# A Performer stage of four interleaved blocks: another order of the steps, and the rotation's sum on another engine

## The chip, the cores and the metric

The kernel runs on one core of a Trainium2 chip. The metric is the device time of the whole program in microseconds (us). A core has five engines that run their own instruction streams in order and meet at semaphores: TensorE (PE, matmuls into PSUM banks; PEld is its weight load), VectorE (DVE), ScalarE (ACT), GpSimd (POOL) and SyncE (SP, which issues the transfers).

## The reference, cut to what matters

A small hybrid network runs on 8 images of 128 channels and 16x16 pixels: an adder convolution, a layer of state-space scans with convolutions, a layer of attention with a mixture of experts, and a Performer of eight layers with a spectral filter at the end. The change lies in the Performer's attention. For each layer, of 8 heads with 16 channels:

```python
q = (t @ Wq[i] + bq[i]).reshape(Bb, N, H, DH).transpose(0, 2, 1, 3)
k = (t @ Wk[i] + bk[i]).reshape(Bb, N, H, DH).transpose(0, 2, 1, 3)
...
q = apply_rotary(q, sin, cos)          # t * cos + rot * sin, rot swaps the pairs
k = apply_rotary(k, sin, cos)
qp = softmax_kernel(q, proj[i], True)  # exp(q @ proj - |q|^2 / 2 - max) + eps
kp = softmax_kernel(k, proj[i], False)
d_inv = 1.0 / jnp.einsum('bhnm,bhm->bhn', qp, jnp.sum(kp, axis=2))
ctx = jnp.einsum('bhnm,bhnd->bhmd', kp, v)
o = jnp.einsum('bhnm,bhmd->bhnd', qp, ctx) * d_inv[..., None]
```

Each attention is followed by a layer norm and a GELU network of 512 hidden channels.

## The kernel before

The 2048 tokens are held channels first, as four blocks of 128x512 numbers in fp32. All of the third layer (attention, experts) and the Performer is written as a generator per block, `_block`, that yields after each step; a step is a handful of instructions on several engines, such as a matmul, the operation that reads its bank, and what belongs to it. A block has 297 steps, 32 for each Performer layer. All four blocks share TensorE, VectorE and ScalarE, and while one block waits for a result another's step should fill the gap.

The order is written out by hand. `AHEAD` runs the first 30 steps of blocks 0 and 1 (the third layer's work) early, beside the convolutions. `ORDER` is a list of 1132 digits: each says which block takes its next step. In this part the instructions stand on every engine's queue exactly in the order in which the steps write them; inside a block the order of steps is fixed. The loads of a layer's weights (`lw`, two buffers) are issued on SyncE's queue by the first block that reaches the layer. ScalarE needs one table of functions for exponential and logarithm and another for GELU and tanh; `act` writes a table load (L1071) where the kind changes along the list.

The names used below, each with its line:

- `xc`, `var`, `u`: the three steps of a layer norm (`_norm`): centring matmul and square, variance matmul with logarithm and exponential, product on VectorE (L1150 or L1154, then L1158).
- `rotated`, for `k` and then `q`, one step each: a matmul into bank `pa`; product with the sines into `ro` (L1386, VectorE); square with bias into `sqk` or `sqq` (ScalarE, L1079 in the helper `act`); product with the cosines into `rk` or `rq` (L1390, VectorE); exchange of neighbouring rows of `ro` (L1392, VectorE); sum of the two (L1394, GpSimd). The query's step also writes `us` (L1401) and two `ub` (L1405) on VectorE.
- `pl`, `dg`: sums of the squares by head, transposed (L1420, L1425).
- `pf` with `mxk`, `ek` (L1435, L1437): four steps of key features; `pm`, `gm`, `dm` (L1452, L1454), `pg`, `vo`: maxima over the tokens and scaling of the values.
- `pq` with `mq`, `ex` (L1484 to L1487): query features; `px`, `qp` (L1494): their transposes; `pc`, `ks`, `ctx` (L1522 to L1524): context; `pn`, `rd` (L1553), `po`, `H` (L1557): output.
- `g` and `p`: the GELU network, ending in `H` (L1346). At the very end `th` and `X` (L1360).
- `m`, `me`, `p` out of `T` and `H`, `g` out of `ug` and `me`: the spectral filter behind the Performer, with transfers of `m`.

Two engines that read the same PSUM bank are put one behind the other in the order in which the program writes them. So in `rotated` the second product waits for the square, and the square waits for the first product.

## Time and profile before

| | |
|---|---|
| three timed runs | median 3227.53 us, 3219.98 to 3228.8 |
| profiled execution | 3226.15 us, its span 3224.3 us |
| busy over the span | PE 2958.1 us (92%), DVE 2517.3 (78%), ACT 2223.2 (69%), POOL 734.7 (23%) |
| Performer stage with the rest of the third layer | about 1850 to 2985 us |
| mean granted clock of TensorE | 0.978 |
| table loads L1071 | 134, 171.9 us |
| GpSimd's sums L1394 | 64, 1.27 us each |

The span is the time from the first to the last instruction. The page of the profile gives the busy time of each engine, the chain of waits (the work that ended last, followed back from the end), and the groups of instructions by line, with the mean duration and the idle time of their engine just before them. The adder convolution fills the first 1000 us, the scans the next 750, the spectral filter the last 240.

### The profile page before, as it was taken

The numbers are of one execution on the slowest core, as the hardware profiler recorded it, in microseconds if no ns is written. First come the engines' busy times: TensorE is split into PE (matmuls) and PEld (weight loads), VectorE is DVE, ScalarE is ACT, GpSimd is POOL, SyncE is SP. The second block draws the span as 40 slices with busy tenths as digits, with TensorE's granted clock in tenths as the row PEclk, the third lists the DMA queues.
The fourth block names the chain that finished last, engine by engine and source line by source line (L and its number), as shares of the span: only waits on it lengthen the run. The fifth ranks groups of instructions, "written<-read, shape, count | busy, mean of one in ns | idle before, by whom it ended". The sixth has DMA issues, their size and how long they took to land.

```text
span 3224.3 us, 42449 instructions
## 1 busy us (share of the span) xinstructions
PE 2958.1 (92%) x16686; PEld 1306.8 (41%) x16686; DVE 2517.3 (78%) x3467; ACT 2223.2 (69%) x2660; POOL 734.7 (23%) x433
## 2 busy tenths in 40 slices
PE   6999999999997778988987988899899899989999
PEld 2333333333332224334333445455455555555444
DVE  6999999999996998999998268767676676774531
ACT  6999999999995777777774234476677667757111
POOL 3000000000002787788785000100000000010110
PEclk9999999999998999999999999999999999989999
DMA  1000000000002434434443000000000000000200
GB/s 38 1 1 5 1 1 4 1 1 5 1 1 99 142 133 139 145 131 142 145 133 109 26 1 1 13 13 1 13 13 1 13 13 1 13 1 8 81 26 13
DMA packets 39195, 131.45 MB, mean 41 GB/s; under 512 B 7490, under 2 KB 10572, under 8 KB 37588
## 3 DMA queue, kind: packets, MB, share of 16 engines
q1 hardware_dynamic: 38564, 128.02, 11.8%
q8 instruction: 131, 2.15, 0.3%
q10 hardware_dynamic: 432, 0.73, 0.1%
q14 instruction: 68, 0.56, 0.1%
HBM read 125.85 MB, written 1.84 MB: 40 GB/s over the span
## 4 chain that ended last, share of the span: by engine, by line
PE 58%; DVE 25%; ACT 10%; POOL 4%; issue 2%; DMA 1%; DVEq 0%; ACTq 0%; POOLq 0%
PE o L265 29%; DVE st L812 8%; PE p L265 5%; DVE hc L821 4%; PE g L265 4%; PE conv L265 3%; ACT L1071 2%; PE acc L265 2%; PE xc L265 2%; POOL dbu L726 1%; PE var L265 1%; PE pn L265 1%; ACT g L1079 1%; PE pf L265 1%; PE pq L265 1%
## 5 line engine op out<-in xcount | busy, mean ns | idle before, releaser
L265 PE MATMUL o<-d,sel 128*32 128x512 f32 x8800 | 946.5, 592 | 5.5 <-DVE d L405 5.5
L407 ACT ACTIVATE d<-sh,w 128x2048 f32<-128x2048 f32 x460 | 886.1, 1996 | 64.7 <-PE o L265 54.6
L405 DVE TENSOR_SCALAR d<-sh,w 128x2048 f32<-128x2048 f32 x640 | 789.5, 1292 | 48.1 <-PE o L265 38.3
L726 POOL TENSOR_TENSOR dbu<-du,bs 128x1024 f32<-128x1024 f32 x191 | 447.0, 2364 | 1018.6 <-DVE du L700 989.8
L265 PEld LDWEIGHTS o<-d,sel 128*32 128x32 f32 x8800 | 299.5, 110 | 651.7 <-issue 540.3
L812 DVE TENSOR_TENSOR_SCAN st<-da,dbu 128x512 f32<-128x512 f32 x384 | 448.0, 1207 | 13.2 <-POOL dbu L726 11.3
L265 PE MATMUL acc<-hc,cst 128*128 128x512 f32 x768 | 379.1, 619 | 83.7 <-DVE hc L821 83.1
L739 ACT ACTIVATE da<-delta,neg_a 128x510 f32<-128x510 f32 x384 | 256.5, 685 | 82.0 <-DVE st L812 81.0
L265 PEld LDWEIGHTS acc<-hc,cst 128*128 128x128 f32 x768 | 137.7, 193 | 293.2 <-DVE hc L821 172.4
L821 DVE TENSOR_TENSOR hc<-st,pcs 128x1024 f32<-128x1024 f32 x192 | 234.5, 1221 | 25.4 <-ACT tok L867 0.5
L1394 POOL TENSOR_TENSOR rk<-rk,ro 128x512 f32<-128x512 f32 x32 | 40.8, 1274 | 824.9 <-DVE ro L1392 506.8
L1071 ACT ACT_TABLE_LOAD x134 | 171.9, 1283 | 2.4
L731 ACT COPY pcs<-cs 128x512 f32<-128x512 f32 x192 | 112.5, 586 | 79.4 <-DVE hc L821 77.9
L1674 ACT COPY ug<-p 128x512 f32<-128x512 f32 x64 | 37.5, 586 | 176.7 <-PE p L265 176.7
L1079 ACT ACTIVATE ex<-ex 128x352 f32<-128x352 f32 x128 | 62.9, 494 | 109.2 <-DVE ex L1487 104.5
L265 PE MATMUL conv<-pad,f 128*128 128x512 f32 x288 | 134.1, 600 | 3.2 <-ACT pad L967 2.1
L265 PE MATMUL p<-u,lw 128*128 128x512 f32 x256 | 124.2, 608 | 3.5 <-DVE u L1158 2.0
L399 DVE SCALAR_TENSOR_TENSOR d<-sh,w,d 128x2048 f32<-128x2048 f32 x52 | 122.3, 2352 | 1.9
L265 PE MATMUL p<-g,lw 128*128 128x512 f32 x256 | 117.7, 603 | 3.4 <-ACT g L1079 3.3
L1079 ACT ACTIVATE ek<-ek 128x352 f32<-128x352 f32 x128 | 61.9, 493 | 80.2 <-DVE ek L1437 79.5
L265 PE MATMUL p<-T,H 128*128 128x512 f32 x256 | 113.6, 596 | 4.0 <-DVE ug L1676 3.7
L265 PE MATMUL g<-ug,me 128*128 128x512 f32 (+1 forms) x320 | 112.0, 509 | 0.0
(315 smaller groups left out, 4081.6 us busy)
## 6 DMA issues: line engine op xcount, KB each, us to landing
bs<-rows SPq DMA_DIRECT2D x96, 512.0 KB, 3.8
cs<-rows SPq DMA_DIRECT2D x96, 512.0 KB, 4.7
m<-in_Mphi SPq DMA_DIRECT2D x8, 1024.0 KB, 4.8
lw<-in_layers SPq DMA_DIRECT2D x8, 948.0 KB, 4.5
f<-in_fuse SPq DMA_DIRECT2D x2, 1152.0 KB, 7.5
T<-in_T SPq DMA_DIRECT2D x1, 2064.0 KB, 7.6
x<-in_x SPq DMA_DIRECT2D x4, 256.0 KB, 5.9
total<-sums SPq DMA_DIRECT2D x16, 64.0 KB, 2.0
```

The costliest lines, as they stand in the source:

```text
L265: self.nc.tensor.matmul(out, lhsT=lhsT, rhs=rhs, start=start, stop=stop)
L399: nc.vector.scalar_tensor_tensor(held, tap(k), w[:, k, f : f + 1], held, ALU.max, ALU.add)
L405: nc.vector.tensor_scalar(d, tap(k), wk, None, ALU.max)
L407: nc.scalar.activation(d, tap(k), AF.Abs, scale=-1.0, bias=wk)
L726: gen.tensor_tensor(dbs[r], got[r // NST]["du"], bc(row("bs", r), 1, 2), ALU.mult)
L731: nc.scalar.copy(pcs[r], row("cs", r))
L739: nc.scalar.activation(das[g % 3][:, :, 1:], d[:, :, 1:], AF.Exp, scale=a)
L812: nc.vector.tensor_tensor_scan(st[:, h, :], da, dbs[r][:, h, :], 0.0, ALU.mult, ALU.add)
L821: nc.vector.tensor_tensor(hc, st, bc(pcs[r][:, :], 1, 2), ALU.mult)
L1071: S.tc.keep_in_program_order(S.nc.scalar.preload_act_table_set(name))
L1079: S.nc.scalar.activation(out, src, func, **kw)
L1394: nc.gpsimd.tensor_add(r, r, o)
```

## The change

Three things change: the list `ORDER`; in `rotated`, both VectorE products are written in a row and the square after them; and the sum of the rotation moves from GpSimd to VectorE. `AHEAD` and everything else stay.

```diff
 ORDER = [int(t) for t in (
-    "2312231312321312320312031032031203103230132103113211301320120032110321112311331010331033013310023123"
...
-    "03232233120202023102321312331022"
+    "3213231232131213023213021023021023121301131131231231023110311131312132113211331313331331030102030213"
...
+    "32330022303003321023122313133021"
 )]
...
         nc.vector.scalar_tensor_tensor(o, pa, bias, bc(S.c("sin"), 1, 2), ALU.add, ALU.mult)
+        nc.vector.scalar_tensor_tensor(r, pa, bias, bc(S.c("cos"), 1, 2), ALU.add, ALU.mult)
 
         sq = many.tile([P, BLK], F32, tag="t", name="sq" + name)
         act(S, sq, pa.rearrange("p b l -> p (b l)"), AF.Square, bias=bias)
-        nc.vector.scalar_tensor_tensor(r, pa, bias, bc(S.c("cos"), 1, 2), ALU.add, ALU.mult)
         o = o.rearrange("p b l -> p (b l)")
         nc.vector.stream_shuffle(o, o, EXCHANGE)
         r = r.rearrange("p b l -> p (b l)")
-        nc.gpsimd.tensor_add(r, r, o)
+        nc.vector.tensor_add(r, r, o)
         return r, sq
```

In the new list block 3 takes the first step, and the counts of steps by block are the same.

## The prediction

> **What bounds the kernel now.** I read the page first, for the stages: TensorE (PE) is 92% busy over the span, but the rotation stands only in the performer stage. So next the windows of that stage, from 1850 to 2985 us (columns: window and length, then busy us and instructions of PE, PEld, DVE, ACT, POOL, then clock, DMA share, GB/s):

> ```profile
> 1850.00:2985.00 1135.00, 1031.78 (x5463) 582.81 (x5464) 794.62 (x1962) 712.77 (x1145) 83.81 (x68) 0.95 0.02 8
> ```

> Three engines are well loaded, none is full. The chain of waits decides: adding its pieces inside this window gives PE 493 us, DVE 370, ACT 243, issue 27. So TensorE is the end less than half of the time, and an edit on DVE can show. The chain around one key rotation:

> ```profile
> 2205.40 1.11 PE pa L265 x2
> ...
> 2206.54 0.76 DVE ro L1386
> ...
> 2207.32 0.70 ACT sqk L1079
> ...
> 2208.04 0.69 DVE rk L1390
> 2208.73 0.71 DVE ro L1392
> 2209.45 0.18 DVE gm L1452
> ...
> 2209.65 1.26 DVE dm L1454
> ```

> The two VectorE products read one bank, and between them DVE stands still for ScalarE's square: product, square, product run one after another. Then come two pieces of another block's step, and `dm`, 16x16 numbers, takes 1.26 us. The timeline says why (start us, us, engine, line; in brackets the idle time before):

> ```profile
> 2209.62 1.27 POOL L1394 TENSOR_TENSOR rk<-rk,ro 128x512 f32<-128x512 f32 x1 [19.97 <-DVE gm L1452]
> 2209.65 1.26 DVE L1454 TENSOR_SCALAR dm<-cst,gm 16x16 f32<-16x16 f32 x1
> ```

> It lasts as long as GpSimd's add (it takes 0.22 in the 29 of 31 cases without an add beside it). Groups by line in the window (count, then busy us and mean ns of one, then idle us just before them and its releaser) and three single lines (ns min/median/max) price all of it:

> ```profile
> L1386 DVE SCALAR_TENSOR_TENSOR ro<-pa,vecs,cst 128x512 f32<-128x512 f32 x64 | 47.5, 742 | 5.5 <-PE pa L265 5.3
> L1390 DVE SCALAR_TENSOR_TENSOR rk<-pa,vecs,cst 128x512 f32<-128x512 f32 x32 | 24.0, 751 | 33.6 <-ACT sqk L1079 33.6
> L1390 DVE SCALAR_TENSOR_TENSOR rq<-pa,vecs,cst 128x512 f32<-128x512 f32 x32 | 24.0, 751 | 30.2 <-ACT sqq L1079 30.2
> L1392 DVE STREAM_SHUFFLE ro<-ro 128x512 f32<-128x512 f32 x64 | 46.5, 726 | 0.0
> L1405 DVE TENSOR_SCALAR ub<-ones,us x64: 251/726/1308, 1936.8 to 2904.4; 128x88 f32<-128x88 f32 x64
> L1485 DVE TENSOR_TENSOR mq<-mq,dg x128: 166/168/1028, 1960.7 to 2942.3; 128x8 f32<-128x8 f32 x128
> L1360 DVE TENSOR_TENSOR X<-X,th x4: 681/692/1122, 2947.8 to 2975.5; 128x512 f32<-128x512 f32 x4
> ```

> **The change part by part.**

> *Second product ahead of the square.* DVE's 64 waits for the square, 33.6 + 30.2 = 63.8 us, go: the listing of built instructions has the second product without a wait. On the chain the squares (sqk 21.1, sqq 19.6) are 40.7 us. The same listing lets the square wait for DVE, so it starts one product, 0.751 us, later. Behind it on ScalarE's queue stand the exponentials, `qp` copies and gelus of other blocks; behind the square itself `pl` on TensorE. ScalarE already waits for the first product 39 times of 64 (21.2 + 23.5 us). I price this at nothing in the forecast, because the written order sets the squares elsewhere too and ScalarE is 63% busy; uncovered, it costs 64 x 0.751 = 48 us (rival B).

> *GpSimd's add leaves.* Each query rotation is followed by `us` and two `ub`. The first `ub` averages 1.283 us, the second 0.253: 32 x 1.030 = 33.0 us in which DVE waits for the add. Other DVE instructions beside an add lose, over their medians without one, 7.7 us (9 of `mq` L1485), 3.9 (4 of `ctx` L1524), 2.1 (2 of `dm`) and 3.4 in a few others: 17.1. Instructions that read one operand from PSUM lose nothing (`ek` is 525 ns without an add beside it and 524 with). After the change GpSimd has nothing in this stage but four copies of 0.62 us, so I take back all 50.1 on DVE. On the chain: `ub` has 34.2 us there, of which 1.030/1.536 is excess, 22.9; of the others I take DVE's share, 370/795 of 17.1, 8.0.

> *DVE's add arrives.* The nearest row is `X<-X,th`, the same form: 0.69 us, its 1.12 being one beside a GpSimd copy. 64 x 0.69 = 44.2 us. It stands right behind the shuffle, and the shuffle has 35.7 of its 46.5 us on the chain, so I charge 44.2 x 0.77 = 33.9. Bounds 0 (none on the chain) and 44.2.

> [...]

> *Table loads.* The built lists hold 134 loads of ScalarE's tables before and 132 after, at 1.283 us; the chain has 78 of their 171.9 us, so 1.2 us.

> *The written order.* All 1132 steps move against each other; every instruction keeps its place inside its block. On SP's queue go with them the seven layer loads (4.5 us to landing): from the third layer on they are issued 46 to 75 steps after the other buffer's last reader, before 40 to 79, so they stay hidden. The first `m` load waits for the third of the four last norms instead of the second, about 2 us later against the end of the stage; 13 us of `p` matmuls cover it, uncovered it costs those 2 us. GpSimd's queue has no step left to be moved past.

> Is the new order better or worse in itself? I added up, for each step, its rows on PE, DVE and ACT (a key rotation: 0.86, 3.2 with its wait, 0.68; PE's at the granted clock of 0.96), cut the list into stretches and took the busiest engine of each. With the old rotation in both orders, stretches of 10, 20, 40 and 80 steps give 1116, 1056, 1032, 1005 us before and 1098, 1026, 1004, 996 after: 9 to 30 less. But spacing has not improved: a step stands at most two places behind its block's last one 348 times before, 355 after, and from `rq` to `pl`, where the need rises from 1.6 to 2.4 us (0.18 matmul tail, products, square), the median TensorE work between falls from 5.2 to 4.2. I take 3 us of gain, and keep 0 to 30.

> **Sum.** On the chain: 40.7 + 22.9 + 8.0 - 33.9 + 1.2 + 3 = 42 us. The profiled execution took 3226.15 us (span 3224.3; the median of the three runs is 3227.53, 1.4 above): 3226 - 42 = 3184. Bounds: were DVE the end everywhere, 63.8 + 50.1 - 44.2 = 70 us; were it nowhere the end, about 1.

> **Rivals.** Below 0.3%, 10 us, a measurement of this kernel can't tell from no change.

> A, both effects whole: DVE ends the stage throughout (70) and the order's balance is all realised (30): 3126. For it: stretches sums with order and rotation together fall from 1056 to 1003. Against: PE has the largest share of the chain. 0.14.

> B, slower: the wait moves to ScalarE. Each square now stands at the head of ScalarE's queue for a second product, with `ex`, `ek`, `qp` and `g` of three blocks behind it that feed TensorE, and DVE's freed time goes idle for lack of inputs. Price 0.751 each: 39 squares that already waited give 29 us, all 64 give 48: 3254 to 3273. It decides if the delay falls on the chain for more than 42/0.751 = 56 of 64 squares. For it: ACT has 243 us of the chain, and squares have waited for DVE in 39 cases. Against: 37% of ScalarE's time is idle. 0.10.

> [...]

> C, slower: DVE becomes the bound, its add costing 34 us on the chain while the stalls that go were slack: 3226 + 34 - 1 = 3259. [...] Against: DVE's occupied time falls by 70 us net, and 370 us of chain are its own. 0.04.

> D, hidden: the freed time is absorbed by TensorE's queue, 92% busy: 3225. Against: that share counts matmul tails (a 128x512 pass takes 0.43 in a row of them, its record 0.60). 0.06.

> That the wait or the GpSimd add stays is excluded by the built list.

> **How the numbers follow.** My forecast has 0.66, its own range 3160 to 3214. Faster: forecast and A, 0.80; same: D, 0.06; slower: B and C, 0.14. The range 3148 to 3224 leaves out B and C and the far half of A, some 0.2.

> **What would show it.** The two products without idle time between them; the first `ub` at 0.25 us like the second; `mq` never near 1 us; adds on DVE at 0.69; GpSimd's busy time down by 81 us; squares waiting for rk and rq; the last performer copies at 2942 instead of 2984 us, and the 240 us behind them unchanged. It is wrong if ScalarE's idle time ahead of squares grows past 90 us with gaps on TensorE's `pl`, or if TensorE's waits at other hand-offs grow: then the order, not the rotation, has decided.

## The result: 94 us faster, far more than forecast

The changed kernel takes 3132.99 us (median of four runs, 3128.4 to 3134.79) against 3227.25 for the kernel before: ratio 0.971, 95% interval 0.9692 to 0.9728. The forecast was 3184 us with a range of 3148 to 3224, so the direction was right and the size was not: the gain is 94 us instead of 42. Rival A, both effects whole at 3126, was the nearest of the cases told in number; its condition, that VectorE ends the stage throughout, is taken up at the end.

The page of the changed kernel (span; busy us, share and instructions of each engine):

```profile
span 3132.5 us, 42365 instructions
...
PE 2921.4 (93%) x16686; PEld 1288.3 (41%) x16686; DVE 2509.3 (80%) x3531; ACT 2218.4 (71%) x2658; POOL 651.5 (21%) x369
```

GpSimd's busy time falls by 83 us, VectorE's by 8. TensorE, which does the same number of matmuls (x16686 before, too), is busy for 37 us less: that is not in any step of the prediction. The stage's window, in the same columns as before (length, busy us of PE, PEld, DVE, ACT, POOL, clock, DMA share, GB/s):

```profile
1850.00:2891.00 1041.00, 994.51 (x5464) 565.00 (x5465) 786.86 (x2025) 707.27 (x1142) 2.55 (x5) 0.99 0.03 9
```

The stage ends at 2891 instead of 2984 us, so it holds all of the gain that can be told. The column to see is the clock, 0.99 instead of 0.95. The groups of the rotation in this window:

```profile
L1387 DVE SCALAR_TENSOR_TENSOR rk<-pa,vecs,cst 128x512 f32<-128x512 f32 x32 | 23.7, 741 | 0.0
L1387 DVE SCALAR_TENSOR_TENSOR rq<-pa,vecs,cst 128x512 f32<-128x512 f32 x32 | 23.7, 741 | 0.0
L1394 DVE TENSOR_TENSOR rq<-rq,ro 128x512 f32<-128x512 f32 x32 | 22.2, 692 | 1.1
L1079 ACT ACTIVATE sqk<-pa,vecs 128x512 f32<-128x512 f32 x32 | 21.9, 684 | 39.1 <-DVE rk L1387 38.4 <-PE p L265 0.7
L1079 ACT ACTIVATE sqq<-pa,vecs 128x512 f32<-128x512 f32 x32 | 21.8, 681 | 25.8 <-DVE rq L1387 24.9 <-PE px L1494 0.9
L1485 DVE TENSOR_TENSOR mq<-mq,dg 128x8 f32<-128x8 f32 x128 | 21.4, 167 | 4.4
L1405 DVE TENSOR_SCALAR ub<-ones,us 128x88 f32<-128x88 f32 x64 | 14.1, 263 | 1.1
```

The second product waits for nothing (0.0 behind the last bar, where 33.6 and 30.2 stood); the sum on VectorE takes 692 ns; `mq` and `ub` have lost their stalls (167 and 263 ns on average). The squares' waits for VectorE have grown from 44.7 to 63.3 us. On VectorE's timeline a rotation is now one piece (start us, us):

```profile
2201.21 0.74 DVE L1386 SCALAR_TENSOR_TENSOR ro<-pa,vecs,cst 128x512 f32<-128x512 f32 x1
2201.88 0.74 DVE L1387 SCALAR_TENSOR_TENSOR rk<-pa,vecs,cst 128x512 f32<-128x512 f32 x1
...
2202.54 0.73 DVE L1392 STREAM_SHUFFLE ro<-ro 128x512 f32<-128x512 f32 x1
2203.31 0.69 DVE L1394 TENSOR_TENSOR rk<-rk,ro 128x512 f32<-128x512 f32 x1
```

### The profile page after: what moved, and what is told of

It reads as the page before. It is cut to its first block, busy times and chain, and to the rows that moved or that the text cites. A ratio compares the mean times of both kernels' runs of the same rounds, so it can differ in the third digit from the quotient of the medians.

```text
span 3132.5 us, 42365 instructions
## 1 busy us (share of the span) xinstructions
PE 2921.4 (93%) x16686; PEld 1288.3 (41%) x16686; DVE 2509.3 (80%) x3531; ACT 2218.4 (71%) x2658; POOL 651.5 (21%) x369
## 4 chain that ended last, share of the span: by engine, by line
PE 64%; DVE 24%; ACT 6%; POOL 4%; issue 2%; DMA 1%; DVEq 0%; ACTq 0%; POOLq 0%
PE o L265 30%; DVE st L812 8%; PE p L265 7%; DVE hc L821 4%; PE g L265 4%; PE conv L265 3%; PE acc L265 2%; PE var L265 2%; PE pf L265 2%; PE xc L265 2%; PE pc L265 2%; PE pq L265 2%; POOL dbu L726 2%; PE pn L265 1%; PE px L1494 1%
## 5 line engine op out<-in xcount | busy, mean ns | idle before, releaser
L265 PE MATMUL o<-d,sel 128*32 128x512 f32 x8800 | 946.5, 592 | 5.5 <-DVE d L405 5.5
L265 PEld LDWEIGHTS o<-d,sel 128*32 128x32 f32 x8800 | 299.1, 110 | 652.1 <-issue 540.6
L265 PE MATMUL acc<-hc,cst 128*128 128x512 f32 x768 | 377.4, 616 | 84.9 <-DVE hc L821 84.4
L265 PEld LDWEIGHTS acc<-hc,cst 128*128 128x128 f32 x768 | 137.1, 192 | 293.4 <-DVE hc L821 173.0
L265 PE MATMUL conv<-pad,f 128*128 128x512 f32 x288 | 133.7, 598 | 4.1 <-ACT pad L967 2.2
L265 PE MATMUL p<-u,lw 128*128 128x512 f32 x256 | 124.0, 608 | 3.7 <-ACT g L1079 2.8
L265 PE MATMUL p<-g,lw 128*128 128x512 f32 x256 | 119.1, 609 | 8.8 <-ACT g L1079 8.8
L265 PE MATMUL p<-T,H 128*128 128x512 f32 x256 | 113.4, 596 | 3.8 <-DVE ug L1676 3.5
L265 PE MATMUL g<-ug,me 128*128 128x512 f32 (+1 forms) x320 | 112.1, 509 | 0.1
L1079 ACT ACTIVATE ex<-ex 128x352 f32<-128x352 f32 x128 | 62.8, 494 | 68.6 <-DVE ex L1487 67.3
L1484 DVE TENSOR_REDUCE mq<-pq 128x8 f32<-128x352 f32 x128 | 66.4, 519 | 41.4 <-PE pq L265 41.0
```

Source lines behind the costliest of these rows:

```text
L265: self.nc.tensor.matmul(out, lhsT=lhsT, rhs=rhs, start=start, stop=stop)
L1079: S.nc.scalar.activation(out, src, func, **kw)
L1484: nc.vector.tensor_reduce(mq, f, AX.X, ALU.max)
```

## The experiments

All numbers stand in one table; the texts below lead through it. "us" is the median of 4 to 10 runs, the columns behind the ratio come from one profiled execution each. The stage is the time from 1850 us to the end of the last performer copy into `H`. TensorE's idle and busy time in it add up to it. "Half clock" is the time in the stage in which the profile's clock record grants TensorE half speed.

The kernel before was run again with each group of experiments: median 3223.6 us with the x kernels, 3227.7 with y and with z7 and z8, 3225.9 with z10, w10, w11 and v12, 3228.9 with w13 and n. The ratios are to these, so a few microseconds between kernels of different groups mean nothing.

| kernel | us | ratio to before (95%) | stage | PE idle | PE busy | half clock |
|---|---|---|---|---|---|---|
| before | 3227.3 | | 1134.2 | 103.2 | 1031.0 | 102.4 |
| x1: new order alone | 3191.5 | 0.9883 to 0.9927 | 1100.2 | 84.6 | 1015.6 | 61.4 |
| x3: old order, products in a row | 3151.3 | 0.9752 to 0.9804 | 1062.1 | 63.0 | 999.1 | 30.7 |
| x4: old order, sum on VectorE | 3218.1 | 0.9975 to 1.0001 | 1121.2 | 99.2 | 1021.9 | 78.5 |
| x2: old order, both | 3150.0 | 0.9751 to 0.9795 | 1058.3 | 62.2 | 996.1 | 20.5 |
| y6: new order, sum on VectorE | 3181.8 | 0.9845 to 0.9880 | 1089.4 | 76.5 | 1012.9 | 54.6 |
| y5: new order, products in a row | 3132.9 | 0.9695 to 0.9737 | 1038.7 | 46.5 | 992.2 | 23.9 |
| after (new order, both) | 3133.0 | 0.9692 to 0.9728 | 1041.1 | 46.5 | 994.6 | 27.3 |
| z7: before, 57 filling matmuls | 3225.8 | 0.9986 to 1.0008 | 1133.4 | 76.9 | 1056.5 | 41.0 |
| z10: before, 32 filling matmuls | 3218.3 | 0.9960 to 0.9988 | 1124.1 | 81.0 | 1043.2 | 61.4 |
| z8: after, idle adds on GpSimd | 3149.9 | 0.9745 to 0.9784 | 1060.7 | 60.0 | 1000.7 | 34.1 |
| w10: after, dead adds on VectorE | 3159.7 | 0.9765 to 0.9820 | 1065.8 | 64.0 | 1001.8 | 34.1 |
| w11: after, small square between | 3200.7 | 0.9889 to 0.9947 | 1110.3 | 90.1 | 1020.2 | 68.3 |
| w13: after, small square behind | 3140.3 | 0.9706 to 0.9735 | 1046.2 | 51.0 | 995.2 | 27.3 |
| v12: after, key's square on GpSimd | 3141.4 | 0.9694 to 0.9764 | 1050.8 | 51.2 | 999.6 | 41.0 |
| n14: before, no table loads | 3198.8 | 0.9884 to 0.9914 | 1108.8 | 92.6 | 1016.1 | 64.9 |
| n15: n14, products in a row | 3143.1 | 0.9709 to 0.9741 | 1052.5 | 56.9 | 995.6 | 30.7 |

**The three edits apart.** x1 takes `ORDER` of the new kernel and the rotation of the old; x2 the other way round; x3 and x4 split x2:

```diff
# x3, under the old order
         nc.vector.scalar_tensor_tensor(o, pa, bias, bc(S.c("sin"), 1, 2), ALU.add, ALU.mult)
+        nc.vector.scalar_tensor_tensor(r, pa, bias, bc(S.c("cos"), 1, 2), ALU.add, ALU.mult)
 ...
         act(S, sq, pa.rearrange("p b l -> p (b l)"), AF.Square, bias=bias)
-        nc.vector.scalar_tensor_tensor(r, pa, bias, bc(S.c("cos"), 1, 2), ALU.add, ALU.mult)
# x4, under the old order
-        nc.gpsimd.tensor_add(r, r, o)
+        nc.vector.tensor_add(r, r, o)
```

x1: 

> The new written order with the old rotation (product, square, product, sum on GpSimd). Theory R (the rotation's stalls are the main cost, the order adds little): 3 to 25 us less than before, about 3205 to 3224, half-clock time after 1850 us still above 80 us. Theory O (the order itself carries the part of the gain that the sum lacked): 50 us or more less, 3175 or below, and half-clock time near the 31 us of the changed kernel.

x2: 

> The old written order with the new rotation (both products, then the square; sum on VectorE). Theory R: the 39 us of the chain sum and some 20 to 35 more through the clock, about 3155 to 3170, half-clock time after 1850 us falling from 104 to about 50 us. Theory O: at most the 39 us of the chain, 3185 to 3200, half-clock time little changed.

x3: 

> The old order; only the second product is put ahead of the square, the sum stays on GpSimd. By the chain sum the squares' 40.7 us leave and nothing comes: 3187. If the wait only moves to ScalarE (rival B of the prediction): 3226 to 3273. If the product's wait was slack that another wait replaces: 3215 to 3230.

x4: 

> The old order; only the sum moves from GpSimd to VectorE, product, square, product stay. By the chain sum 22.9 + 8.0 come back and 33.9 are paid: 3223 to 3232, no change. [...] If VectorE is the bound and the stalls were slack: 3250 or more.

Against 3223.6 us for the kernel before in these runs, the order alone gives 32 us, more than theory R allowed and less than theory O. Both edits of the rotation give 74, 5 us beyond theory R's range, and the half clock falls further than it said, to 20.5 us. x3 alone gives 72, outside all three cases told for it: the exchange of square and second product is nearly all of the 74, and its term of 40.7 us was far too small. The moved sum gives 5 us alone, 5 us below the case by the chain sum, with an interval that touches no change, and 1 us on top of the exchange.

The window of x3 says where the 72 us are:

```profile
1850.00:2912.00 1062.00, 999.00 (x5461) 565.49 (x5462) 787.57 (x1962) 711.52 (x1144) 83.94 (x68) 0.99 0.03 8
```

Same matmuls, but TensorE busy 999 us instead of 1031, and the clock back at 0.99. Of the 72.1 us by which the stage is shorter, 40.2 are TensorE's idle time and 31.9 its busy time. The half-clock time is 71.7 us less. In the changed kernel's trace 128x512 passes start 0.86 us apart in a spell of half clock at 2186 us and 0.43 behind it, twice the time in the spell. So 71.7 us less of half clock can shorten the busy time by up to half of that, 35.9 us, and the 31.9 fit. Over all kernels of the table with the same matmuls, busy time goes with the half-clock time: from x2 to before, 34.9 us for 81.9, or 0.43 us each, and between 0.3 and 0.5 for the others against before.

**The other half of the table.** y5 and y6 repeat x3 and x4 under the new order.

y5: 

> The new order with both products ahead of the square, but the sum still on GpSimd. From the single edits under the old order (square 72 us, sum 5 and 1 us): the sum is worth next to nothing, 3131 to 3140. If the new order was made for the sum on VectorE, it is worth more here: 3145 to 3160.

y6: 

> The new order with the sum on VectorE, but product, square, product as before. If the edits act alike under both orders, the sum gives 3 to 8 us on the 3191 of the new order alone: 3183 to 3190. If the new order needs the sum there: 3165 to 3180.

y5 is as fast as the changed kernel: under the exchange, the sum's engine makes no difference (0.1 us). y6 gains 10 us on x1, a little over the first case's range, as x4 did on before. The exchange is worth 59 us on x1 (to y5) and 49 on y6 (to the changed kernel). So the parts overlap: exchange 72, then the sum 1, then the order 17. Unrounded these make 90.6 us; the 3.6 that lack to 94.3 are the distance between the kernel before in these runs, 3223.6, and beside the result, 3227.3.

**Is the clock a cause or a sign?** The clock record of the kernel before shows how a spell of half clock begins. Four windows of 3.41 us:

```profile
2433.27:2436.68 3.41, 1.99 (x26) 1.00 (x28) 2.48 (x5) 1.22 (x3) 1.27 (x1) 1.00 0.01 2
2436.68:2440.09 3.41, 1.78 (x34) 0.80 (x26) 3.37 (x8) 2.76 (x5) 1.27 (x1) 1.00 0.00 0
2440.09:2443.51 3.42, 3.42 (x11) 1.73 (x12) 0.99 (x3) 1.62 (x3) 0.00 (x0) 0.51 0.00 0
2443.51:2446.92 3.41, 3.41 (x14) 1.74 (x12) 2.56 (x6) 0.92 (x2) 0.00 (x0) 1.00 0.00 0
```

TensorE is busy for 1.78 of 3.41 us in the second; in the third, though it never pauses, it is granted 0.51 of its clock; then it is back. Runs of this one kernel differ in the same sense: of the 13 runs beside the x kernels, the five with a mean granted clock of 0.983 to 0.986 had spans of 3211.8 to 3219.4 us, the four with 0.977 to 0.979 spans of 3224.8 to 3227.2. That they go together doesn't tell which is the cause. To test it, z7 adds useless matmuls of a constant into the bank of those 35 steps before which TensorE stood idle for over 1 us:

```diff
...   # n comes from a list by step, 1 to 4; `full` is the whole bank
+    for _ in range(n):
+        S.mm(full, S.center, S.cst[:, 0:BLK])
...
```

z7: 

> The kernel before, with useless matmuls of a constant (57 of 128x512 in 35 steps, about 49 us of TensorE time at full clock) put ahead of the steps at which the trace of before shows TensorE idle for over 1 us; nothing waits for their result, and the bank is overwritten by the step's own matmul. Theory C (the half-clock spells are a cause: TensorE idle in a 3.4 us stretch halves its clock in the next): the gaps are filled, half-clock time after 1850 us falls from 102 to below 60 us, and the kernel gets 10 to 25 us faster although it does more work, 3200 to 3215. Theory S (the spells are a mere sign of waiting and cost nothing by themselves): 0 to 49 us slower, 3225 to 3275.

The time is unchanged, at the lower end of theory S and out of theory C's range, though 49 us of work were added: half-clock time falls by 61 us and idle time by 26. The trace shows that in 14 of the 35 steps the filling itself had to wait for its bank, so it came after the gap. z10 leaves those out:

z10: 

> The kernel before with useless matmuls only in the 21 of the 35 steps where, in the trace of the first filled kernel, they did not have to wait for their bank: 32 of 128x512, 27.5 us of TensorE work. Theory C (half-clock spells are a cause): the 21.5 us of work that only stood behind a bank are gone, the clock gain stays: 3200 to 3213, faster than before with more work. Theory S (spells cost nothing by themselves): 3225 or above.

```profile
1850.00:2974.00 1124.00, 1043.04 (x5529) 584.97 (x5528) 794.96 (x1962) 712.81 (x1145) 84.53 (x69) 0.97 0.02 8
```

With 27.5 us more for TensorE to do (32 of 0.86), the kernel is 8 us faster (interval 0.9960 to 0.9988). Its idle time falls by 22 us and its half-clock time by 41. That is less than theory C's 13 to 26, but theory S has no room for a gain: part of the price of an idle gap is paid in the matmuls behind it. The gain is small and rests on one placement of the filling; that the filling also helps by moving other steps in time is not excluded.

**What a microsecond of VectorE is worth.** z8 brings GpSimd's adds back beside VectorE without use for them, w10 gives VectorE a useless add:

```diff
# z8
         nc.vector.tensor_add(r, r, o)
+        nc.gpsimd.tensor_add(o, o, o)
# w10
         nc.vector.tensor_add(r, r, o)
+        nc.vector.tensor_add(o, o, o)
```

z8: 

> The changed kernel, in which GpSimd adds the exchanged product, no longer needed, to itself right after each sum on VectorE: 64 adds of 1.27 us that nothing needs but a later use of the buffer. It brings the stalls of VectorE beside GpSimd back without giving anything. By the chain sum 22.9 + 8.0 = 31 us slower, about 3164. If the stalls were mostly slack under the new rotation: 3135 to 3145.

w10: 

> The changed kernel with one more add on VectorE after each rotation's sum, of dead data (0.69 us, 64 times, 44 us of VectorE time). Theory D (VectorE's freed time is what the exchange of square and product brought; 64 us gave 58 to 74): 40 to 50 us slower, 3173 to 3183. Theory Q (it was the tie to ScalarE's queue, VectorE's time alone is worth a third, as with GpSimd's stalls): 13 to 20 us slower, 3146 to 3153.

In z8 the adds come back, and one of two `ub` is again held up to 1.04 us (groups, then one line):

```profile
L1395 POOL TENSOR_TENSOR ro<-ro 128x512 f32<-128x512 f32 x64 | 66.7, 1042 | 920.9 <-DVE rk L1394 546.2 <-DVE ks L1523 113.8 <-DVE rq L1394 99.0
```

```profile
L1406 DVE TENSOR_SCALAR ub<-ones,us x64: 251/264/1037, 1939.7 to 2839.5; 128x88 f32<-128x88 f32 x64
```

VectorE loses 35 us to them (its busy time in the stage grows from 786.9 to 822.3), and the kernel 17: between the two expectations. In w10, 44 us of work (64 of 0.69) cost 27, between the two as well. So in the changed kernel a microsecond of VectorE was worth 0.5 to 0.6. At that price the 63.8 us of waiting that the exchange removed under the old order would be 32 to 38 us; it brought 72. Under the new order it removed 61.6 us of waiting from y6, 31 to 37 us at that price, and brought 49. VectorE's time alone explains half to three quarters, if its price is the same in the kernels that still have the wait, which was not measured.

**The tie between two queues.** w11 puts VectorE's wait back without the square's length: a square of one column stands between the products, and the whole square stays behind them. w13 is its control, with the same small square behind both.

```diff
# w11: ahead of the second product; w13: behind it
+        touch = many.tile([P, 1], F32, tag="touch", name="touch" + name)
+        act(S, touch, pa[:, 0, 0:1], AF.Square, bias=bias)
```

w11: 

> The changed kernel with a one-column square of the bank (on ScalarE, its result unused) between the two products, and the whole square behind them as changed: VectorE must again wait in the middle for ScalarE's queue, but not for the 0.68 us of a whole square. Theory D (only VectorE's blocked time counts): the wait is some 0.3 us where ScalarE is free, 20 to 30 us in all, 15 to 25 us slower, 3148 to 3158. Theory Q (the tie to whatever stands ahead on ScalarE's queue counts): 40 us or more slower, 3173 to 3195.

w13: 

> The control of the kernel with a one-column square between the products: the changed kernel with the same 64 small squares on ScalarE, but written after both products, so VectorE waits for none of them. Theory Q (the tie of VectorE to ScalarE's queue made the 68 us): 3133 to 3145. If the 16 us of extra work on ScalarE made them: 3180 to 3200.

w11's groups:

```profile
L1389 DVE SCALAR_TENSOR_TENSOR rq<-pa,vecs,cst 128x512 f32<-128x512 f32 x32 | 24.0, 751 | 29.4 <-ACT touchq L1079 29.4
L1389 DVE SCALAR_TENSOR_TENSOR rk<-pa,vecs,cst 128x512 f32<-128x512 f32 x32 | 24.0, 750 | 23.4 <-ACT touchk L1079 23.4
L1079 ACT ACTIVATE sqk<-pa,vecs 128x512 f32<-128x512 f32 x32 | 22.0, 687 | 26.2 <-DVE rk L1389 26.2
...
L1079 ACT ACTIVATE touchk<-pa,vecs 128x1 f32<-128x1 f32 x32 | 8.2, 257 | 22.5 <-DVE ro L1386 22.3
```

An instruction of 0.26 us makes VectorE wait for 52.8 us, and the kernel loses 68 us (3132.99 to 3200.73), more than theory Q's range. The same small squares without the wait cost 7 us (w13), as theory Q said. So 60 us come with the wait, 1.14 us for each microsecond of it, twice what VectorE's work costs.

That is not the price of the tie that the exchange removed. y6 has the same order and the same sum as w11, but the whole square between the products:

```profile
L1390 DVE SCALAR_TENSOR_TENSOR rq<-pa,vecs,cst 128x512 f32<-128x512 f32 x32 | 24.0, 751 | 26.1 <-ACT sqq L1079 26.1
L1390 DVE SCALAR_TENSOR_TENSOR rk<-pa,vecs,cst 128x512 f32<-128x512 f32 x32 | 24.0, 751 | 35.5 <-ACT sqk L1079 35.5
```

Its VectorE waits longer, 61.6 us, and yet it is 19 us faster than w11; by it the tie costs 49 us, 0.79 for each microsecond of waiting (under the old order, x3: 72 for 63.8, 1.13). In w11 ScalarE stops twice for a rotation instead of once, and the whole square comes later than in either kernel. TensorE waits for it at `pl` (total us, times, longest; the changed kernel, then w11; in y6 16.6 us):

```profile
PE pl L265 <- ACT sqq L1079: 6.6, 9, 1.7
PE pl L265 <- ACT sqq L1079: 27.0, 20, 3.5
```

So a wait at the head of ScalarE's queue cost more than the same time spent working, by a factor between 1.3 and 2.3. Theory Q offers a reason: while VectorE waits (52.8 us in w11), all other blocks' steps behind on VectorE wait too, and ScalarE waits for VectorE in turn (there 22.3 us ahead of `touchk`, 26.2 ahead of `sqk`). The runs agree with it, but how the cost divides between the two queues, and how much of w11's is the later square, is not shown.

**Do the table loads make the tie?** n14 and n15 put an identity in the place of GELU and tanh, so those functions are left out and no table is changed in the stage.

```diff
     elif func in (AF.Gelu, AF.Tanh):
-        tables(S, GELU)
+        func = AF.Identity
```

n14: 

> The kernel before without the changes of ScalarE's tables in the stage: GELU and tanh are left out (an identity of the same size stands in their place), so 132 of 134 loads of 1.283 us go, 169 us of ScalarE's time. The chain has 78 us of loads: 3140 to 3155 by that; if the gaps that they make on TensorE and its clock go too: 3080 to 3130.

n15: 

> The same without table loads, and both products ahead of the square; its difference to the kernel without loads is to be read. Theory L (a good part of the tie is that loads and what they delay stand ahead of the square): the exchange is worth 20 to 45 us here instead of 72. If it is the 0.68 us of the square and its place alone: 60 to 75 us, as with the loads.

132 loads, 169 us of ScalarE's time and 78 us of the chain, are worth 30 us: far less than expected. Without them the exchange is still worth 56 us, in between the two ranges. So some 17 of its 72 us hang on the loads, by theory L as they stand ahead of squares; most of the tie needs no loads.

**A try at a faster version.** v12 takes the key's square on GpSimd from the rotated key:

```diff
-        act(S, sq, pa.rearrange("p b l -> p (b l)"), AF.Square, bias=bias)
+        if name == "q":
+            act(S, sq, pa.rearrange("p b l -> p (b l)"), AF.Square, bias=bias)
...
         nc.vector.tensor_add(r, r, o)
+        if name == "k":
+            nc.gpsimd.tensor_tensor(sq, r, r, ALU.mult)
```

v12: 

> A try at a faster version: the changed kernel, but the key's square is taken by GpSimd from the rotated key in SBUF (a rotation keeps the sum of squares of a pair). ScalarE loses 32 squares (22 us) and the 38 us that it stood waiting for VectorE before them; 32 GpSimd operations of 1.27 us bring half of the stalls beside GpSimd back (8 us by the kernel with idle adds). By theory Q: 5 to 20 us faster, 3113 to 3128. If ScalarE is no longer near the end: 5 to 10 us slower, 3138 to 3143.

It is 8 us slower than the changed kernel, with intervals that overlap: no gain, and the case told by theory Q fails. ScalarE's wait for VectorE ahead of the query's square has grown from 24.9 to 49.1 us, so at least part of the time that the key's squares left free was spent waiting there. Nothing run here beats the changed kernel by more than can be told apart.

## Why the prediction was wrong in size

- *The bound.* Right: the stage holds the whole gain, and an edit on VectorE shows. The chain in the stage now has 640 us of TensorE, 279 of VectorE, 104 of ScalarE (before 493, 370, 243): work left the chain on both other engines.
- *Second product ahead of the square.* The failing step. It was priced at the squares' own 40.7 us on the chain; measured alone it is 72, on x1 59. Two things were missing. What stood on ScalarE ahead of a square was on the chain because of the tie: in x3 ScalarE's part of the chain in the stage fell from 243 to 114 us, and its table loads from 78 to 29.5 without one load less. And the gaps cost clock: 31.9 of x3's 72.1 us are shorter busy time of TensorE for the same matmuls. Taken first, the exchange makes 32 of the 52 us that the sum lacked.
- *The square waits longer.* Right to price at nothing. Rival B's ground was there, ScalarE waits 63.3 us for VectorE ahead of squares, but in x3 it cost nothing that shows: TensorE's wait at `pl` for the query's square fell from 9.1 to 4.0 us. Its test, idle time over 90 us, was not met. The other sign of being wrong did appear at one place: TensorE's waits for the GELU's output ahead of `p` grew from 4.1 to 11.5 us. They are 7.8 in x3 under the old order, too, and TensorE's idle time as a whole halved, so they don't say that the order has decided.
- *GpSimd's add leaves, VectorE's arrives.* That 30.9 back and 33.9 paid nearly cancel was right, though not the sign: 5 to 10 us of gain without the exchange, 0 to 1 with it. In the changed kernel each side measures less: stalls of 35 us cost 17, adds of 44 us cost 27. The duration, 0.69 us, was exact. (`dm` is short in 30 of 32 cases of the kernel before, not in 29 of 31; nothing hangs on it.)
- *The table loads.* Two fewer for 1.2 us can't be seen; by n14, a load is worth 30/132 = 0.23 us on average.
- *The written order.* Taken at 3 us with 0 to 30 kept. It is 32 alone and 17 on top of the rest, so this term failed as well: 14 of the missing 52 us. The sums over stretches (9 to 30) were the better guide; the spacing of steps, which spoke against, misled. Which feature of the new order gains the time was not tested.
- *The sum.* Shares of one chain were added as if each were a price. Runs gave 72 for 40.7, 17 for some 31, 27 for 33.9, 30 for 78. The upper bound counted at most the 63.8 us of waiting for the exchange, which brought 72: what the waits cost beyond VectorE's own time, on TensorE's clock among others, stood in no term. The range left out the far half of rival A, and the result lies there. Rival A's number was near by luck: VectorE does not end the stage throughout (279 of 1041 us of the chain), and its 70 + 30 us stand where the runs have 74 and 17.
- *C and D* fell: VectorE's share of the chain went down instead of up, and the gain was not hidden behind TensorE.

## What to carry to other kernels

Where two engines read one PSUM bank, write all reads of one engine in a row if the work allows: an alternation ties two queues together, and here a microsecond of it cost 0.8 to 1.1, one of VectorE's work 0.5 to 0.6. A share of the chain tells where to look, not what an edit is worth; here edits were worth 0.4 to 1.8 times their share, and one run with the edit alone tells. Where TensorE has idle gaps of a microsecond or two, look at the granted clock behind them: in this kernel 0.43 us of busy time went with each microsecond of half clock.
